# One GpSimd instruction for two states and two chunks in a selective-scan block

## The chip, the cores and the metric

The kernel runs on one core of one Trainium2 chip. The metric is the device time of one execution in microseconds (us), lower is better. Before the change it is 4063.8 us, the median of 3 runs (4062.99 to 4069.68).

## What is computed

The reference is a stack of four layers over `x` of 4 x 512 x 256 numbers, all in fp32: a cross-attention block, a transformer block with self- and cross-attention and a gated feed-forward part, a stack of four Mamba blocks over a 64-token prefix and the 512 tokens, and another transformer block. The change lies in the Mamba layer alone. Its core, cut down:

```python
def mamba_block(x, ip_w, cw, cb, xp_w, dtp_w, dtp_b, A_log, Dp, op_w):
    ...
    dt = jax.nn.softplus(jnp.einsum('bsr,er->bse', dt, dtp_w) + dtp_b)
    A = -jnp.exp(A_log)
    dA = jnp.exp(dt[..., None] * A)
    dBu = dt[..., None] * Bm[:, :, None, :] * xi[..., None]

    def step(h, t):
        da, dbu, c = t
        h = da * h + dbu
        return (h, jnp.einsum('bes,bs->be', h, c))
    ...
    y = ys.transpose(1, 0, 2) + xi * Dp
    y = y * jax.nn.silu(z)
    return jnp.einsum('bse,de->bsd', y, op_w)
```

`e` runs over 512 channels, `s` over 16 states, and there are four such blocks and four sequences.

## The kernel before

Layers 0 and 1 run first, with the 64 prefix tokens of the Mamba layer computed beside them; then comes the Mamba layer over the 512 tokens (`layer2`, called the scan block here), then layer 3. In the scan block the 512 channels are four chunks of 128 partitions, and time (512 steps) lies along the free dimension.

The work is cut into 16 units (4 blocks x 4 sequences). A unit has two pairs of chunks, a pair has 8 groups of two states, and a group has two chunks `k`. One pass `i` of the main loop, of 512, is one chunk of one group: `i = 32 n + 16 pair + 2 s2 + k`, and its group is `i // 2`. I call such a pass a slot. The order of all instructions is written out by hand (`tc.manual_schedule()`): each engine runs its own in program order, and waits only where data or a buffer demand it. A slot's steps:

- `maps`: SyncE loads the rows of B and C for two states, spread over 128 partitions (`bB`, 2 buffers, and `bC`, 4 buffers), 6 and 4 slots ahead.
- `decay` (L1706): ScalarE computes exp(dt A) of both states into PSUM (`ps_dA`, two buffers), one slot ahead.
- `product` (L1692): GpSimd multiplies dt x by B for one state and both chunks into `dBu` ([128, 2 states, 512, 2 chunks], chunks innermost, 3 buffers), three slots ahead. `begin` (L1711): ScalarE writes the first element of each state, from the state left by the prefix.
- `states` (L1718): VectorE scans both states of a chunk, reading `ps_dA` and, with a stride of two, `dBu`. The result goes back into `ps_dA`, or into an SBUF tile `hP` where GpSimd makes the output product.
- output products with C: `outputs_here` (L1723) on VectorE into `hC`, in the same slot, or `outputs` (L1727) on GpSimd in place in `hP`, one slot later. `on_gpsimd(i)` picks 13 slots in 32: the even ones without 10, 20 and 30. `hC` and `hP` share 6 buffers.
- `add_up` (L1749): TensorE transposes the products of a chunk by 8 matmuls with the identity, and thereby adds them up over the states in PSUM (`ps_y`), two slots later for VectorE's and three for GpSimd's. For a pair's first chunk 16 matmuls come before them (L1738, `dD` times `xi`, the term with D), which start the sums. `close_pair` (L1765) multiplies the sums by the gate on VectorE two slots after a pair's last chunk, into `g`.

Everything else of the layer is taken along by generators that `advance()` moves on twice a slot: `front` (norm, input projection `ps_in`, convolution `ps_cv`, `ps_x`, two units ahead), `step` (dt by `ps_dt`, softplus, `dtx`), `gate` (`ps_z`, into `zs`), `gated` (transposes of `g`, output projection `ps_out`, and the addition to `hT_res` on VectorE at L1633), and, in the last block, `tokens` (the final norm; L1667 on VectorE scales 256 columns with two operands in SBUF). They share two PSUM banks. `flush_silu` runs a silu on ScalarE, with its table loads, in slots 10 and 14 of a unit. The first part of the main loop's order:

```python
                    if main and i + 3 < NU * US:
                        product(i + 3)
                    if 0 <= i - 1 < NU * US:
                        outputs(i - 1)
                    ...
                    if main:
                        states(i)
                    ...
                    for j in (i - 3, i - 2):
                        if 0 <= j < NU * US and on_gpsimd(j) == (j == i - 3):
                            add_up(j)
```

Of the kernel before, what the change touches and what calls it, by code (L numbers as in the profile page):

```python
# [8 lines left out]
F32 = mybir.dt.float32  # L9
AF = mybir.ActivationFunctionType  # L10
ALU = mybir.AluOpType
# [4 lines left out]
P = 128  # L16
B = 4
T = 512
# [97 lines left out]
        return not (any(self.queues) or self.norms or self.pend or self.aside)  # L116


def on_gpsimd(i):

    return i % 2 == 0 and i % 32 not in (10, 20, 30)


@with_exitstack
def kernel(ctx: ExitStack, tc: tile.TileContext, t: dict, out: bass.AP):
    nc = tc.nc
# [1242 lines left out]
    def layer2(hT, A, far, h63, tail, X, fw, wl, late):  # L1369
# [5 lines left out]
        with ExitStack() as st:  # L1375
            pool = st.enter_context(tc.tile_pool(name="a2", bufs=1))
# [3 lines left out]
            NU = L * B  # L1380
            PS = 2 * (NS // 2)
            US = 2 * PS
# [40 lines left out]
            units = [{} for _ in range(NU)]  # L1423
# [248 lines left out]
            bmap, dBus, dAs, hCs, ysum = {}, {}, {}, {}, {}  # L1672

            def where(i):
                n, r = divmod(i, US)
                pair, r = divmod(r, PS)
                s2, k = divmod(r, 2)
                return n, pair, s2, k
# [5 lines left out]
                nc.sync.dma_start(out=tl, in_=units[n]["scr"][k, 2 * s2 : 2 * s2 + 2].partition_broadcast(P))  # L1684
                bmap[i // 2, k] = tl

            def product(i):
                n, pair, s2, j = where(i)
                dtx = units[n]["got", pair][1]
                if j == 0:  # L1690
                    dBus[i // 2] = pool.tile([P, 2, T, 2], F32, name="dBu", tag="dBu", bufs=3)
                nc.gpsimd.tensor_mul(  # L1692
                    dBus[i // 2][:, j, 1:, :],
                    dtx[:, 1:, :],
                    bmap[i // 2, 0][:, j, 1:].unsqueeze(2).broadcast_to([P, T - 1, 2]),
                )

            def decay(i, j):
# [6 lines left out]
                dt = units[n]["got", pair][0][:, k, :]  # L1705
                nc.scalar.activation(dA, dt, AF.Exp, scale=A[:, l, m, s : s + 1])  # L1706

            def begin(i):
                n, pair, s2, k = where(i)
                h0 = units[n]["got", pair][2]  # L1710
                nc.scalar.copy(dBus[i // 2][:, :, 0, :], h0[:, :, 2 * s2 : 2 * s2 + 2].rearrange("p k s -> p s k"))  # L1711

            def states(i):
                hCs[i] = hC = pool.tile([P, 2, T], F32, name="hP" if on_gpsimd(i) else "hC", tag="hC", bufs=6)
                dA = dAs[i].rearrange("p s t -> p (s t)")
                to = hC.rearrange("p s t -> p (s t)") if on_gpsimd(i) else dA
                dBu = dBus[i // 2].rearrange("p s t k -> p (s t) k")[:, :, i % 2]
                nc.vector.tensor_tensor_scan(to, dA, dBu, 0.0, ALU.mult, ALU.add)  # L1718

            def outputs_here(i):  # L1720
                dA = dAs.pop(i)
                if not on_gpsimd(i):
                    nc.vector.tensor_mul(hCs[i], dA, bmap[i // 2, 1])  # L1723

            def outputs(i):
                if on_gpsimd(i):
                    nc.gpsimd.tensor_mul(hCs[i], hCs[i], bmap[i // 2, 1])  # L1727

            def add_up(i):
                n, pair, s2, k = where(i)  # L1730
# [36 lines left out]
            def advance():  # L1767
                for gen in list(active):
                    try:
                        next(gen)  # L1770
                    except StopIteration:
                        active.remove(gen)
# [13 lines left out]
            with tc.manual_schedule():  # L1786
                for i in range(first, last):
                    n, r = divmod(i, US)
# [16 lines left out]
                    main = 0 <= i < NU * US  # L1805
# [3 lines left out]
                    for k, ahead in ((0, 6), (1, 4)):  # L1809
                        j = i + ahead  # L1810
# [8 lines left out]
                    if i == -1:  # L1819
                        product(0)  # L1820
                        product(1)
                        product(2)
                        begin(0)
                    if main and i + 3 < NU * US:
                        product(i + 3)
                    if 0 <= i - 1 < NU * US:
                        outputs(i - 1)

                    e = i - LAG
                    closing = 0 < e <= NU * US and e % PS == 0  # L1830
# [4 lines left out]
                    if main:  # L1835
                        states(i)
                    if closing:

                        advance()
                        advance()  # L1840
                    for j in (i - 3, i - 2):
                        if 0 <= j < NU * US and on_gpsimd(j) == (j == i - 3):
                            add_up(j)
                    if not closing:
                        advance()
                    if main:
                        outputs_here(i)
                    if main and i % 2 == 0 and i + 2 < NU * US:
                        begin(i + 2)
                    if not closing:  # L1850
                        advance()
                assert not active and len(banks) == 2
# [137 lines left out]
    with ExitStack() as st:  # L1990
        xp = st.enter_context(tc.tile_pool(name="X3", bufs=1))
        X = xp.tile([P, NT, D], F32, name="X")
        fw = row(xp, "l2_fw")
        wl = st.enter_context(tc.tile_pool(name="w2", bufs=1))
        wa = {}

        def late():

            wa["q"] = load_w(wl, "L3_q", [P, DC, 512], tag="inx")
            ko = wl.tile([P, 2, 1024], F32, name="w_ko", tag="dg")  # L2000
            wa["v"] = load_w(wl, "L3_v", [P, DC, D], tag="dD", bufs=2)
            for k, n in enumerate("ko"):
                wa[n] = ko[:, k, :].rearrange("p (c n) -> p c n", c=(DC, 4)[k])
                nc.sync.dma_start(out=wa[n], in_=t[f"L3_{n}"].rearrange("(c p) n -> p c n", p=P))

        layer2(hT, A, far[:, 0:2], h63, tail, X, fw, wl, late)
        layer3(X, wa, wl)
# [70 lines left out]
```

## Time and profile before

| | |
|---|---|
| median of 3 runs | 4063.8 us (4062.99 to 4069.68) |
| the profiled execution's own time | 4068.3 us |
| its span in the profile | 4066.5 us |
| granted TensorE clock | 0.914 |
| busy share of the span: PE, DVE, ACT, POOL | 86%, 72%, 53%, 60% |
| scan block | 1598 us to 3354 us after the start |
| input products on GpSimd (L1692) | 512 of 2136 ns |
| output products on GpSimd (L1727) | 208 of 2365 ns |
| scans on VectorE (L1718) | 304 of 2283 ns and 208 of 2279 ns |
| output products on VectorE (L1723) | 304 of 1223 ns |

The profile is of one execution. PE is TensorE's matmuls, PEld its weight loads, DVE VectorE, ACT ScalarE, POOL GpSimd, SP SyncE. A group of instructions has its line, engine and operation, what it writes and reads, shapes and count; after the bar stand its busy time, the mean ns of one, the idle time of the engine just before, and what ended that. A row of the waits has who waited, for whom, and the total, the times and the longest in us. A row of the timeline has start, length, engine, line, and the idle time before it in brackets. A line can be a helper's: TensorE's L190 and L183 are `matmul_k` and its version in halves.

### The profile page before, as it was taken

The page shows a single profiled execution, that of the slowest core. Times are in us where ns is not written, and L with a number is a line of the kernel's source. Part 1 is how long each engine was busy: PE and PEld are TensorE (multiplying, and loading weights), DVE is VectorE, ACT ScalarE, POOL GpSimd, SP SyncE. Part 2 cuts the span into 40 slices and gives each one's busy share as a digit, 9 for nine tenths or more (in the row PEclk, how much of TensorE's full clock was granted, in tenths as well). Part 3 has the DMA queues.
Part 4 walks back from the last instruction along what each step waited for, and adds up shares of the span by engine and source line. Part 5 has one row for each costly group of instructions (what it writes and reads, how often), then busy time and mean ns, then how long its engine had stood idle before and what let it go on. Part 6 is the DMA issues. An engine that isn't in the chain of part 4 may idle for free. (4 is left out here: it accounts for less than half of the span.)

```text
span 4066.5 us, 48201 instructions
## 1 busy us (share of the span) xinstructions
PE 3492.8 (86%) x17616; PEld 2200.1 (54%) x17616; DVE 2942.0 (72%) x2821; ACT 2156.9 (53%) x4106; POOL 2440.9 (60%) x1585
## 2 busy tenths in 40 slices
PE   7989998998888897888888888888888568999889
PEld 4654554544565554555555555555555444555446
DVE  5547567566565642889999989999999995676653
ACT  2345455454322433666767767666676643566422
POOL 3349269077100424899999999999999981000131
PEclk8999999999988998988988898889988778999999
DMA  2023022023100112444544545454444441000000
GB/s 77 12 87 104 25 81 96 18 90 104 45 1 0 54 31 70 151 157 154 164 166 156 162 157 176 156 163 156 164 158 146 152 142 41 1 1 1 1 6 16
DMA packets 140492, 370.30 MB, mean 91 GB/s; under 512 B 20640, under 2 KB 38240, under 8 KB 140256
## 3 DMA queue, kind: packets, MB, share of 16 engines
q1 hardware_dynamic: 136896, 363.98, 27.4%
q10 hardware_dynamic: 3360, 3.25, 0.3%
q8 instruction: 139, 2.28, 0.2%
q14 instruction: 97, 0.79, 0.1%
HBM read 363.89 MB, written 3.28 MB: 90 GB/s over the span
## 5 line engine op out<-in xcount | busy, mean ns | idle before, releaser
L1692 POOL TENSOR_TENSOR dBu<-dtx,bB 128x1022 f32<-128x1022 f32 x512 | 1084.7, 2136 | 13.0 <-DVE ps_dA L1718 5.9
L1706 ACT ACTIVATE ps_dA<-dt,A 128x512 f32<-128x512 f32 x1024 | 710.7, 694 | 358.1 <-DVE hC L1723 306.9
L1718 DVE TENSOR_TENSOR_SCAN ps_dA<-ps_dA,dBu 128x1024 f32<-128x1024 f32 x304 | 693.9, 2283 | 72.3 <-ACT ps_dA L1706 69.4
L1718 DVE TENSOR_TENSOR_SCAN hP<-ps_dA,dBu 128x1024 f32<-128x1024 f32 x208 | 474.1, 2279 | 58.9 <-POOL dBu L1692 49.8
L1727 POOL TENSOR_TENSOR hP<-hP,bC 128x1024 f32<-128x1024 f32 x208 | 491.9, 2365 | 26.9 <-DVE hP L1718 26.8
L1024 ACT ACTIVATE pr<-ps_s,nm 128x512 f32<-128x512 f32 x512 | 346.0, 688 | 259.8 <-DVE nm L1020 259.7
L1020 DVE TENSOR_REDUCE nm<-ps_s 128x2 f32<-128x1024 f32 x256 | 301.3, 1218 | 158.9 <-PE ps_s L1009 144.8
L1723 DVE TENSOR_TENSOR hC<-ps_dA,bC 128x1024 f32<-128x1024 f32 x304 | 371.7, 1223 | 17.9 <-PE ps_in L190 0.4
L1749 PE MATMUL ps_y<-ident,hC 128*128 128x128 f32 x2432 | 354.4, 296 | 27.3 <-DVE hC L1723 27.1
L1749 PE MATMUL ps_y<-ident,hP 128*128 128x128 f32 x1664 | 263.2, 311 | 110.7 <-POOL hP L1727 110.5
L1749 PEld LDWEIGHTS ps_y<-ident,hC 128*128 128x128 f32 x2432 | 309.9, 154 | 66.9 <-DVE hC L1723 41.8
L1038 PE MATMUL ps_pt<-ident,pr 128*128 128x128 f32 x2048 | 284.5, 279 | 66.8 <-DVE pT L1043 34.0
L1749 PEld LDWEIGHTS ps_y<-ident,hP 128*128 128x128 f32 x1664 | 227.5, 162 | 198.2 <-POOL hP L1727 140.7
L1038 PEld LDWEIGHTS ps_pt<-ident,pr 128*128 128x128 f32 x2048 | 231.9, 142 | 164.6 <-issue 60.6
L668 POOL TENSOR_TENSOR ln_rstd<-ln_rstd,const 128x4 f32<-128x4 f32 x24 | 24.4, 1017 | 446.3 <-DVE ln_rstd L667 444.8
L587 DVE TENSOR_TENSOR_SCAN phb<-pdA,phb 128x512 f32<-128x512 f32 x128 | 225.7, 1778 | 59.0 <-POOL phb L577 42.8
L183 PE MATMUL ps_cv<-xp,w_dg 128*128 128x512 f32 x512 | 239.2, 603 | 26.0 <-ACT xp L1501 19.6
L1041 ACT COPY pT<-ps_pt 128x512 f32<-128x512 f32 x256 | 140.7, 593 | 171.5 <-PE ps_pt L1038 171.1
L1057 PE MATMUL ps_o<-pT,V 128*64 128x256 f32 (+1 forms) x2048 | 221.8, 393 | 1.8 <-ACT AT L1075 1.8
L1009 PE MATMUL ps_s<-kT,qT 64*128 64x512 f32 (+1 forms) x1024 | 209.6, 647 | 2.2 <-DVE kT L1230 1.4
L577 POOL TENSOR_TENSOR phb<-hT_res,pm 128x512 f32<-128x512 f32 x128 | 187.8, 1471 | 34.2 <-DMA pm<-scrp 21.3
L840 POOL TENSOR_TENSOR pr<-pr,rs 128x512 f32<-128x512 f32 x64 | 65.4, 1042 | 218.2 <-DVE rs L838 212.3
(275 smaller groups left out, 6345.8 us busy)
## 6 DMA issues: line engine op xcount, KB each, us to landing
bB<-scr SPq DMA_DIRECT2D x256, 512.0 KB, 3.9
bC<-scr SPq DMA_DIRECT2D x256, 512.0 KB, 4.8
pm<-scrp SPq DMA_DIRECT2D x224, 256.0 KB, 3.1
w_pw_in<-in_L_in SPq DMA_DIRECT2D x7, 512.0 KB, 4.6
X<-in_x SPq DMA_DIRECT2D x4, 512.0 KB, 7.7
w_L_W<-in_L_W SPq DMA_DIRECT2D x2, 1024.0 KB, 10.0
w_L_Wq<-in_L_Wq SPq DMA_DIRECT2D x2, 1024.0 KB, 6.4
w_L_Wo<-in_L_Wo SPq DMA_DIRECT2D x2, 1024.0 KB, 8.9
```

The costliest lines, as they stand in the source:

```text
L183: nc.tensor.matmul(dst, l, r, start=(i == 0), stop=(i == len(pairs) - 1))
L587: nc.vector.tensor_tensor_scan(hb, dA, hb, 0.0, ALU.mult, ALU.add)
L1020: nc.vector.tensor_reduce(nm, ps, AX.X, ALU.max, negate=True)
L1024: nc.scalar.activation(pr, ps[:, x, :], AF.Exp, bias=nm[:, x : x + 1], accum_out=rs[:, y : y + 1])
L1038: nc.tensor.transpose(pp[:, t4, :], pr[:, t4 * P : (t4 + 1) * P], ident)
L1057: nc.tensor.matmul(ps_o[0][j * stride : (j + 1) * stride, half * W2 : (half + 1) * W2], Vs[n][0][:, t4, h * stride : (h + 1) * stride], pT ...
L1692: nc.gpsimd.tensor_mul(dBus[i // 2][:, j, 1:, :], dtx[:, 1:, :], bmap[i // 2, 0][:, j, 1:].unsqueeze(2).broadcast_to([P, T - 1, 2]),)
L1706: nc.scalar.activation(dA, dt, AF.Exp, scale=A[:, l, m, s : s + 1])
L1718: nc.vector.tensor_tensor_scan(to, dA, dBu, 0.0, ALU.mult, ALU.add)
L1723: nc.vector.tensor_mul(hCs[i], dA, bmap[i // 2, 1])
L1727: nc.gpsimd.tensor_mul(hCs[i], hCs[i], bmap[i // 2, 1])
L1749: nc.tensor.matmul(y[:, j, k * P : (k + 1) * P], hC[:, s, j * P : (j + 1) * P], ident, is_transpose=True, start=False, stop=(2 * s2 + s == ...
```

## The change

`product` and `outputs` now take a group `g` instead of a slot. One instruction makes both states and both chunks of an input product, with `dtx` repeated over the states and B over the chunks. Where a group is GpSimd's, the scans of both chunks write their states in place in `dBu`, and one instruction multiplies these by C, repeated over the chunks, also in place; TensorE's weight loads then read a chunk of `dBu` with a stride of two. `on_gpsimd` picks whole groups: 0, 2 and 4 of eight, and group 30 of 32, so 13 of 32. `dBu` has 4 buffers instead of 3, `hC` 4 instead of 6, and `hP` is gone. The input product of a group is issued in one slot, three before its first scan; the output product two slots after the group's first scan; GpSimd's chunks are added up four slots after their scan instead of three.

```diff
--- before.py
+++ after.py
@@ -116,9 +116,9 @@
         return not (any(self.queues) or self.norms or self.pend or self.aside)
 
 
-def on_gpsimd(i):
-
-    return i % 2 == 0 and i % 32 not in (10, 20, 30)
+def on_gpsimd(q):
+
+    return q % 8 in (0, 2, 4) or q % 32 == 30
 
 
 @with_exitstack
@@ -1684,15 +1684,13 @@
                 nc.sync.dma_start(out=tl, in_=units[n]["scr"][k, 2 * s2 : 2 * s2 + 2].partition_broadcast(P))
                 bmap[i // 2, k] = tl
 
-            def product(i):
-                n, pair, s2, j = where(i)
-                dtx = units[n]["got", pair][1]
-                if j == 0:
-                    dBus[i // 2] = pool.tile([P, 2, T, 2], F32, name="dBu", tag="dBu", bufs=3)
+            def product(g):
+                n, pair, s2, _ = where(2 * g)
+                dBus[g] = pool.tile([P, 2, T, 2], F32, name="dBu", tag="dBu", bufs=4)
                 nc.gpsimd.tensor_mul(
-                    dBus[i // 2][:, j, 1:, :],
-                    dtx[:, 1:, :],
-                    bmap[i // 2, 0][:, j, 1:].unsqueeze(2).broadcast_to([P, T - 1, 2]),
+                    dBus[g][:, :, 1:, :],
+                    units[n]["got", pair][1][:, 1:, :].unsqueeze(1).broadcast_to([P, 2, T - 1, 2]),
+                    bmap[g, 0][:, :, 1:].unsqueeze(3).broadcast_to([P, 2, T - 1, 2]),
                 )
 
             def decay(i, j):
@@ -1705,26 +1703,28 @@
                 dt = units[n]["got", pair][0][:, k, :]
                 nc.scalar.activation(dA, dt, AF.Exp, scale=A[:, l, m, s : s + 1])
 
-            def begin(i):
-                n, pair, s2, k = where(i)
+            def begin(g):
+                n, pair, s2, _ = where(2 * g)
                 h0 = units[n]["got", pair][2]
-                nc.scalar.copy(dBus[i // 2][:, :, 0, :], h0[:, :, 2 * s2 : 2 * s2 + 2].rearrange("p k s -> p s k"))
+                nc.scalar.copy(dBus[g][:, :, 0, :], h0[:, :, 2 * s2 : 2 * s2 + 2].rearrange("p k s -> p s k"))
 
             def states(i):
-                hCs[i] = hC = pool.tile([P, 2, T], F32, name="hP" if on_gpsimd(i) else "hC", tag="hC", bufs=6)
                 dA = dAs[i].rearrange("p s t -> p (s t)")
-                to = hC.rearrange("p s t -> p (s t)") if on_gpsimd(i) else dA
                 dBu = dBus[i // 2].rearrange("p s t k -> p (s t) k")[:, :, i % 2]
-                nc.vector.tensor_tensor_scan(to, dA, dBu, 0.0, ALU.mult, ALU.add)
+                nc.vector.tensor_tensor_scan(dBu if on_gpsimd(i // 2) else dA, dA, dBu, 0.0, ALU.mult, ALU.add)
 
             def outputs_here(i):
                 dA = dAs.pop(i)
-                if not on_gpsimd(i):
-                    nc.vector.tensor_mul(hCs[i], dA, bmap[i // 2, 1])
-
-            def outputs(i):
-                if on_gpsimd(i):
-                    nc.gpsimd.tensor_mul(hCs[i], hCs[i], bmap[i // 2, 1])
+                if not on_gpsimd(i // 2):
+                    hCs[i] = hC = pool.tile([P, 2, T], F32, name="hC", tag="hC", bufs=4)
+                    nc.vector.tensor_mul(hC, dA, bmap[i // 2, 1])
+
+            def outputs(g):
+                if on_gpsimd(g):
+                    h = dBus[g]
+                    nc.gpsimd.tensor_mul(h, h, bmap[g, 1].unsqueeze(3).broadcast_to([P, 2, T, 2]))
+                    for k in range(2):
+                        hCs[2 * g + k] = h[:, :, :, k]
 
             def add_up(i):
                 n, pair, s2, k = where(i)
@@ -1819,12 +1819,11 @@
                     if i == -1:
                         product(0)
                         product(1)
-                        product(2)
                         begin(0)
-                    if main and i + 3 < NU * US:
-                        product(i + 3)
-                    if 0 <= i - 1 < NU * US:
-                        outputs(i - 1)
+                    if main and i % 2 and i + 3 < NU * US:
+                        product((i + 3) // 2)
+                    if i % 2 == 0 and 0 <= i - 2 < NU * US:
+                        outputs((i - 2) // 2)
 
                     e = i - LAG
                     closing = 0 < e <= NU * US and e % PS == 0
@@ -1838,15 +1837,15 @@
 
                         advance()
                         advance()
-                    for j in (i - 3, i - 2):
-                        if 0 <= j < NU * US and on_gpsimd(j) == (j == i - 3):
+                    for j in (i - 4, i - 2):
+                        if 0 <= j < NU * US and on_gpsimd(j // 2) == (j == i - 4):
                             add_up(j)
                     if not closing:
                         advance()
                     if main:
                         outputs_here(i)
                     if main and i % 2 == 0 and i + 2 < NU * US:
-                        begin(i + 2)
+                        begin((i + 2) // 2)
                     if not closing:
                         advance()
                 assert not active and len(banks) == 2
```

## The prediction

> **What bounds the kernel now.** I read the slices first, then the windows, the groups of the scan block by shape, the waits of the same stretch, and last the timeline of a few slots. I call one pass `i` of the main loop a slot (512 of them) and 32 slots a unit.
>
> ```profile
> DVE  5547567566565642889999989999999995676653
> POOL 3349269077100424899999999999999981000131
> 1650.00:3100.00 1450.00, 1238.25 (x5703) 831.12 (x5704) 1328.13 (x783) 1011.66 (x1623) 1418.38 (x795) 0.87 0.49 159
> ```
>
> The slices place the scan block: first scan 1598 us, last 3354 us after the start. The window row gives, after its length, busy time of PE, PEld, DVE, ACT, POOL. Of 1450 us GpSimd works 1418 (97.8%), VectorE 1328 (91.6%), TensorE 1238 (85.4%). GpSimd looks like the bound.
>
> ```profile
> L1692 POOL TENSOR_TENSOR dBu<-dtx,bB 128x1022 f32<-128x1022 f32 x512 | 1084.7, 2136 | 13.0 <-DVE ps_dA L1718 5.9
> L1727 POOL TENSOR_TENSOR hP<-hP,bC 128x1024 f32<-128x1024 f32 x208 | 491.9, 2365 | 26.9 <-DVE hP L1718 26.8
> L577 POOL TENSOR_TENSOR phb<-hT_res,pm 128x512 f32<-128x512 f32 x128 | 187.8, 1471 | 34.2 <-DMA pm<-scrp 21.3
> ```
>
> ```profile
> DVE ps_dA L1718 <- ACT ps_dA L1706: 55.7, 55, 2.4
> DVE hT_res L1633 <- PE ps_out L183: 35.3, 26, 2.6
> DVE ps_dA L1718 <- POOL dBu L1692: 2.5, 3, 0.9
> PE ps_y L1749 <- POOL hP L1727: 64.9, 29, 3.9
> PE ps_y L1738 <- DVE g L1765: 41.5, 14, 4.1
> ```
>
> The waits (1650 to 3100 us; total, times, longest) say otherwise. VectorE waits 2.5 us for GpSimd's input products, but 55.7 for ScalarE's decays and 35.3 for TensorE. GpSimd's output products hold TensorE (64.9). So a faster GpSimd reaches the end only by way of TensorE. The timeline shows what TensorE does there:
>
> ```profile
> 2598.54 2.27 DVE L1718 TENSOR_TENSOR_SCAN ps_dA<-ps_dA,dBu 128x1024 f32<-128x1024 f32 x1
> ...
> 2601.41 1.04 PE L1749 MATMUL ps_y<-ident,hP 128*128 128x128 f32 x8
> ...
> 2602.28 1.04 PE L1749 MATMUL ps_y<-ident,hC 128*128 128x128 f32 x8
> 2603.16 1.88 PE L190 MATMUL ps_z<-w_inz,hn 128*128 128x512 f32 x4
> ...
> 2604.87 3.60 PE L183 MATMUL ps_out<-gT,w_out 128*128 128x512 f32 x8
> ...
> 2608.51 0.69 DVE L1633 TENSOR_TENSOR hT_res<-ps_out,hT_res 128x512 f32<-128x512 f32 x1 [2.05 <-PE ps_out L183]
> ```
>
> From slot 5 (scan at 2598.54) TensorE has no gap, is 2.9 us behind VectorE, and VectorE then waits 2.05 us for it. TensorE paces slots 3 to 9 of a unit and much of 17 to 31; VectorE and ScalarE pace 10 to 16.
>
> **The change, part by part.** The sum is made against the profiled execution: span 4066.5, its own time 4068.3, 4.5 us above the median of 4063.8. Units take 106.5 to 108.8 us (scan to scan, 32 apart), 115 in the two that hold the final norm. Some 15 units run steadily. A measurement of this kernel tells 0.2% (8 us) from no change.
>
> *GpSimd's instructions.* 512 input products become 256 of twice the size, 208 output products 104. Rows with two full operands give the fixed part: 251 ns at 32 elements (L1578) and 2365 at 1024, so 2.13 ns an element and 183 fixed. L1692, whose B is repeated over two chunks, leaves (2136-183)/1022 = 1.91 ns. The new input product is then 183+2044x1.91 = 4.09 us against 4.27, the new output product, with the same repeat, 4.10 against 4.73: 256x0.18+104x0.63 = 113 us less work. If nothing of the fixed part is saved it is 47. I take 113, as four row sizes lie on that line (L577's shortest, 1257 ns at 512, gives 1274). In the Trainium skill, GPSIMD Engine Reference, section 3.1, a two-input GpSimd operation of 2048 elements is listed at 4497 ns, with no gain for a repeated operand. By that page GpSimd would do about 35 us more instead of less (an estimate from the page), which speaks against the change; the 2136 ns of L1692 is already under half of the page's figure, so I follow the row. On the path I credit the 113 us with nothing: VectorE waited 2.5 us. What is late next is TensorE.
>
> *The buffer of a group on GpSimd.* The states stay in `dBu`, so it comes free after TensorE has added up the second chunk, not after VectorE's second scan. Input product g+4 takes the buffer of g: it is issued in slot 2g+5, and the add it needs opens slot 2g+5 on TensorE. This new wait of GpSimd on TensorE has the output product of g+2 and input product g+5 queued behind it, and for these TensorE, then VectorE (slot 2g+10), wait. In the timeline above the add that would free it ends at 2602.45, 3.9 us after slot 5 began. Then 4.09+4.10+4.09 and about 0.2 of handing over: input product 5 is there 16.4 us after slot 5. VectorE reached slot 10 at 2617.15, 18.6 us after; alone it would need 13.9 (three scans of 2.28, then two chunks at 3.5, in the new order). So in the first half of a unit TensorE's own pace covers the wait; where the cover is gone it costs up to 2.5 us. In slots 25 to 29, where TensorE starts 3.6 to 4.0 late, I count 0.5 us a unit: +8. Bounds 0 and +46 (3 us a unit).
>
> *Which groups go to GpSimd.* Before, even slots but 10, 20 and 30; after, both chunks of groups 0, 2, 4 of eight and one more in 32: 208 products either way. But slots 10 to 15 now all belong to VectorE, which had given away 12 and 14: two products of 1.22 us, +2.44 a unit, +37 over 15 units. Those that leave slots 5 and 9 lie where VectorE waits for TensorE, and bring nothing. Bounds 0 (later slots give it back) and +37; nearest is the stretch itself, which VectorE paces, so +37.
>
> *ScalarE.* At slot 14 a silu and two table loads delay the decay of slot 15; in every unit I looked at the scan there waits 1.75 us. Slot 14 becomes 1.22 longer, so this cover grows: -1.22x15 = -18. The softplus at slot 19 (1.08 us) keeps its distance, since slots 16 to 19 together are as long as before. Bounds 0 and -26.
>
> *The adds one slot later.* TensorE's first adds of a pair, with 16 matmuls before them that wait for `g` (41.5 us, 14 times), move from slot 3 to 4. Four `ps_z` matmuls (1.88 us) of slot 3 now fill that idle time, and the stretch behind it has no gap: -1.88x15 = -28. Bounds -45 (all idle time) and 0.
>
> *The final norm.* L1667 reads two SBUF operands and each of its instructions in the scan block ends with a GpSimd instruction: 9.37 us for four at 3211.93, 0.48 each once GpSimd is quiet. With GpSimd instructions of 4.1 us, four may take up to 16.4, +7 in each of three batches; VectorE's stop also stops GpSimd, so I take +5, +15. Bounds 0 and +21.
>
> *Costs I set at nothing.* The scans write with a stride of two: `hP` 2279 and `ps_dA` 2286 ns already differ only by 7, reads of `dBu` have this stride now, and L587 scans in place over its second input (1191 ns at 512 elements when alone). `hC` falls from 6 to 4 buffers: the fourth chunk back is added up two slots before, and TensorE is at most 6.2 us late. SP's loads are the same 512; the buffer of `bB` is free 4.1 us before its next use where two input products follow each other, landing takes 3.9, so at most some 0.5 us where GpSimd has time. ScalarE's `begin` waits for the same add as the input product, a slot later. TensorE's weight loads of GpSimd's 208 chunks are strided; no row has such a load. Bounded by none and by twice the present 8x0.13 us of a group: 0 to +216 of TensorE's time, half of it hidden at most. I take 0: VectorE and GpSimd rows show no price for this stride. In the Trainium skill, SBUF — State Buffer, under Door 1: The DMA port swizzle, fp32 may be strided within a 16-byte line without loss. No run here shows it for weight loads.
>
> Sum: 0+8+37-18-28+15 = +14 us, so 4082 for the profiled execution and 4063.8+14 = 4078 for the median.
>
> **The rivals.** *GpSimd's relief reaches the end* (faster). For it: 97.8% busy, and TensorE's 64.9 us of waits for output products in 1450. Over 15 units that is some 72 us; with the final norm's +15 it is -57, less what the burst costs: about -45, 4019. Against it: VectorE's own work and its table loads stay. It decides if TensorE's waits for GpSimd were what made it late in slots 17 to 31.
>
> *The new wait of GpSimd for TensorE sets the pace* (slower still). Price 3 us a unit, +46 on top of the +14: 4124. It decides when VectorE would cover slots 5 to 10 in under 16.4 us; 18.6 was measured, and every gain elsewhere brings it closer. Strided weight loads at a price add to the same queue.
>
> *The merged instruction saves nothing* (GpSimd's row stays proportional): GpSimd does 47 us less rather than 113; with credit zero the time stays near the forecast, 4080.
>
> **How the numbers follow.** Forecast with its bounds, the third rival in it, 0.45; relief reaches the end 0.28; the new wait decides 0.27. The forecast's own range is 4050 to 4110, of which I give 0.05 to faster by over 0.2%, 0.15 to within it, 0.25 to slower. Faster 0.28+0.05 = 0.33, same 0.15, slower 0.27+0.25 = 0.52. The range reaches from 4018 (relief) to 4135 (new wait and something of the strided loads); about 0.08 is left out below, 0.1 above.
>
> **What would show it.** L1692's successor at 4.09 us x256 and the output product at 4.10 x104 show the first step; 4.27 or 4.5 shows it wrong. POOL waiting for `PE ps_y` is the new buffer wait; tens of us on VectorE for `dBu` mean that it sets the pace. VectorE's wait at slot 15 should fall to 0.5 us, TensorE's wait for `g` by half, L1667 rise to some 3.5 us. Weight loads of `dBu` above 0.16 us would show a price of the stride. The forecast is wrong if units fall under 106 us or rise over 110.

## The result, and the profile after

| | before | after |
|---|---|---|
| median, same chip | 4063.39 us (4 runs, 4062.29 to 4069.68) | 4119.64 us (4 runs, 4118.49 to 4122.01) |
| ratio, 95% interval | | 1.0136 [1.0118, 1.0153] |
| the profiled execution's own time, span | 4068.3, 4066.5 us | 4122.0, 4120.0 us |
| granted TensorE clock | 0.914 | 0.908 |

The kernel became slower by 56 us. The page of the changed kernel, the slices of VectorE and GpSimd first, then groups of the scan block (busy time, mean ns of one, idle time before and what ended it):

```profile
DVE  5548577576555633898989888988898996766653
POOL 3349168076100425898888988898988881000131
...
L1690 POOL TENSOR_TENSOR dBu<-dtx,bB 128x2044 f32<-128x2044 f32 x256 | 1042.7, 4086 | 46.8 <-DMA bB<-scr 31.2
...
L1725 POOL TENSOR_TENSOR dBu<-dBu,bC 128x2048 f32<-128x2048 f32 x104 | 425.3, 4089 | 162.3 <-issue 120.6
L1714 DVE TENSOR_TENSOR_SCAN dBu<-ps_dA,dBu 128x1024 f32<-128x1024 f32 x208 | 465.1, 2273 | 56.9 <-POOL dBu L1690 49.0
...
L1749 PEld LDWEIGHTS ps_y<-ident,hC 128*128 128x128 f32 x2432 | 311.6, 156 | 145.9 <-DVE hC L1720 130.1
...
L1749 PEld LDWEIGHTS ps_y<-ident,dBu 128*128 128x128 f32 x1664 | 233.7, 209 | 106.5 <-issue 56.8
```

In the scan block the rows of nines of VectorE and of GpSimd are now eights and nines. The two GpSimd instructions last what the sum gave them. GpSimd has less to do (2343.7 us against 2440.9 in the whole span) and now stands idle longer before them: 46.8 and 162.3 us, against 13.0 and 26.9 in the prediction's lines. The window of 1650 to 3100 us shows the same (length, then busy time of PE, PEld, DVE, ACT, POOL, then the granted clock):

```profile
1650.00:3100.00 1450.00, 1215.12 (x5506) 803.57 (x5505) 1286.61 (x754) 972.63 (x1563) 1288.66 (x476) 0.86 0.47 155
```

GpSimd fell from 1418 to 1289 us, but VectorE fell too, from 1328 to 1287, and its work per unit has not shrunk. So VectorE stands longer. The waits of that stretch say for whom (total, times, longest):

```profile
DVE ps_dA L1714 <- ACT ps_dA L1704: 65.9, 76, 4.4
...
PE ps_rb L1472 <- POOL rstd L1465: 54.4, 12, 9.4
...
PE ps_z L190 <- ACT zs L1600: 41.3, 10, 4.8
...
DVE hT_res L1633 <- PE ps_out L183: 39.6, 13, 3.5
...
POOL dBu L1690 <- DMA bB<-scr: 26.4, 13, 2.6
...
DVE g L1765 <- PE ps_y L1749: 22.3, 9, 5.6
...
DVE hn L1479 <- PE ps_rb L1472: 11.5, 4, 2.9
...
PE ps_y L1749 <- POOL dBu L1725: 6.5, 7, 1.5
```

TensorE's wait for GpSimd's output products is nearly gone (64.9 to 6.5), and its wait for `g` (41.5) is not in the list any more. In their place stand a wait for ScalarE's `zs` and one for GpSimd's `rstd`, the small root of the norm. The view of before has for these:

```profile
PE ps_rb L1472 <- POOL rstd L1465: 18.1, 3, 6.0
...
PE ps_z L190 <- ACT zs L1600: 10.9, 13, 2.9
```

The largest new wait of TensorE, 66.2 us for VectorE's `hC` (9.7 before), is not what slows the kernel: in the faster version with earlier adds, below, it is 79.0. VectorE waits longer for three results of TensorE: for `hT_res` 39.6 us against 35.3, for `g` 22.3 against 9.3, for `hn` 11.5 where there was none.

Two tables worked out from the traces, means of eight steady units (slots 96 to 352), in us, with the scan block as a whole in the last column of the first; the experiments are explained below:

| kernel | unit | VectorE busy | GpSimd busy | scan block |
|---|---|---|---|---|
| before | 107.5 | 98.8 | 105.9 | 1755.9 |
| after | 111.7 | 99.1 | 99.8 | 1806.1 |
| groups only | 111.9 | 99.1 | 106.1 | 1801.0 |
| inputs only | 107.3 | 98.8 | 103.5 | 1750.4 |
| after, adds earlier | 108.4 | 99.0 | 99.7 | 1760.8 |
| the same, 14 of 32 | 106.3 | 97.5 | 101.8 | 1734.3 |
| before, 14 of 32 | 110.0 | 97.7 | 108.2 | 1778.7 |

VectorE's idle time is a unit less its busy time: 8.7 us before, 12.6 after. That difference is the slowdown (3.9 us of the 4.2 a unit).

The second table shows where in a unit the time lies: how long VectorE takes from one scan to a later one. The first row has the lengths before, the others how much longer or shorter each stretch is.

| kernel | slots 0-5 | 6-7 | 8-9 | 10-15 | 16-27 | 28-29 | 30-31 | unit |
|---|---|---|---|---|---|---|---|---|
| before | 19.4 | 8.2 | 6.9 | 20.2 | 39.3 | 6.5 | 7.1 | 107.5 |
| after | 0.0 | +3.4 | -1.9 | +2.6 | +0.1 | 0.0 | 0.0 | +4.2 |
| groups only | +1.1 | +0.5 | -1.8 | +2.6 | -0.3 | +2.3 | +0.1 | +4.4 |
| groups only, 12 of 32 | +0.4 | +0.8 | -1.9 | +2.8 | -0.3 | +2.5 | 0.0 | +4.3 |
| after, root left out | +0.3 | +3.0 | -1.9 | +2.7 | -0.8 | -0.5 | 0.0 | +2.7 |
| after, opening matmuls earlier | +0.3 | +1.6 | -1.9 | +2.6 | -0.3 | -0.3 | 0.0 | +2.0 |
| after, adds earlier | -0.1 | +0.2 | -1.9 | +2.6 | -0.1 | +0.1 | 0.0 | +0.9 |
| the same, groups spread | 0.0 | +0.2 | +0.5 | +0.2 | -0.3 | +0.1 | 0.0 | +0.8 |
| adds earlier, 14 of 32 | -1.0 | 0.0 | -1.9 | +1.3 | -0.1 | +0.5 | 0.0 | -1.2 |

The change lengthens two stretches. Slots 6 and 7 hold VectorE's longest wait for TensorE's `ps_out`; in slots 10 to 15 VectorE now makes all the products, and slots 8 and 9 give most of that back.

### The profile page after: what moved, and what is told of

Its sections match the earlier page's. It is cut to its first block, busy times and chain, and to the rows that moved or that the text cites. A ratio compares the mean times of both kernels' runs of the same rounds, so it can differ in the third digit from the quotient of the medians.

```text
span 4120.0 us, 47410 instructions
## 1 busy us (share of the span) xinstructions
PE 3508.2 (85%) x17616; PEld 2197.0 (53%) x17616; DVE 2940.4 (71%) x2821; ACT 2151.2 (52%) x4106; POOL 2343.7 (57%) x1225
## 5 line engine op out<-in xcount | busy, mean ns | idle before, releaser
L1690 POOL TENSOR_TENSOR dBu<-dtx,bB 128x2044 f32<-128x2044 f32 x256 | 1042.7, 4086 | 46.8 <-DMA bB<-scr 31.2
L1714 DVE TENSOR_TENSOR_SCAN ps_dA<-ps_dA,dBu 128x1024 f32<-128x1024 f32 x304 | 696.1, 2290 | 88.3 <-ACT ps_dA L1704 88.2
L1725 POOL TENSOR_TENSOR dBu<-dBu,bC 128x2048 f32<-128x2048 f32 x104 | 425.3, 4089 | 162.3 <-issue 120.6
L1714 DVE TENSOR_TENSOR_SCAN dBu<-ps_dA,dBu 128x1024 f32<-128x1024 f32 x208 | 465.1, 2273 | 56.9 <-POOL dBu L1690 49.0
L1749 PE MATMUL ps_y<-ident,hC 128*128 128x128 f32 x2432 | 363.4, 299 | 92.8 <-DVE hC L1720 92.2
L1749 PEld LDWEIGHTS ps_y<-ident,dBu 128*128 128x128 f32 x1664 | 233.7, 209 | 106.5 <-issue 56.8
L1749 PE MATMUL ps_y<-ident,dBu 128*128 128x128 f32 x1664 | 247.5, 294 | 45.6 <-POOL dBu L1725 45.6
L190 PE MATMUL ps_z<-w_inz,hn 128*128 128x512 f32 x256 | 150.0, 717 | 77.9 <-ACT zs L1600 49.1
```

Of the source, the lines that this page charges most:

```text
L190: nc.tensor.matmul(dst, a, b, start=(i == 0), stop=(i == n - 1))
L1690: nc.gpsimd.tensor_mul(dBus[g][:, :, 1:, :], units[n]["got", pair][1][:, 1:, :].unsqueeze(1).broadcast_to([P, 2, T - 1, 2]), bmap[g, 0][:, ...
L1714: nc.vector.tensor_tensor_scan(dBu if on_gpsimd(i // 2) else dA, dA, dBu, 0.0, ALU.mult, ALU.add)
L1725: nc.gpsimd.tensor_mul(h, h, bmap[g, 1].unsqueeze(3).broadcast_to([P, 2, T, 2]))
L1749: nc.tensor.matmul(y[:, j, k * P : (k + 1) * P], hC[:, s, j * P : (j + 1) * P], ident, is_transpose=True, start=False, stop=(2 * s2 + s == ...
```

## The experiments

Ratios are against the kernel before on the same chip, with 95% intervals. The whole change is +56 us by the medians; 0.001 is 4.07 us.

**Only the distribution.** The kernel before with one line changed: GpSimd takes whole groups; all instructions, slots and buffers stay.

```diff
 def on_gpsimd(i):
-    return i % 2 == 0 and i % 32 not in (10, 20, 30)
+    q = i // 2
+    return q % 8 in (0, 2, 4) or q % 32 == 30
```

> The kernel before with one line changed: whole groups (0, 2, 4 of eight and 30 of 32) give their output products to GpSimd, instead of every second slot. All instructions keep their old size. Theory A (the new distribution over the slots is what costs: VectorE's run of slots 10 to 15, two short slots in a row elsewhere): most of the +56 us appears, 4095 to 4120. Theory B (the doubled GpSimd instructions cost, by what is queued behind them): within 10 us of before, 4055 to 4075.

Measured: 4116.07 us, 1.0115 [1.0098, 1.0132], +47. The waits of this run:

```profile
DVE ps_dA L1719 <- ACT ps_dA L1707: 85.9, 63, 4.9
...
PE ps_cv L184 <- POOL xp L1497: 43.4, 22, 3.4
```

The second line stands at 1.8 us before, and in the waits of after TensorE's matmuls have no such entry. The timeline from slot 27 to slot 30 of a unit shows it (start, length, engine, line, idle time before in brackets; L1693 is the input product, L1728 the output product):

```profile
2473.24 2.13 POOL L1693 TENSOR_TENSOR dBu<-dtx,bB 128x1022 f32<-128x1022 f32 x1
...
2475.32 2.36 POOL L1728 TENSOR_TENSOR hP<-hP,bC 128x1024 f32<-128x1024 f32 x1
...
2477.62 0.20 POOL L1497 COPY xp<-tail 128x3 f32<-128x3 f32 x1
...
2477.87 5.37 PE L184 MATMUL ps_cv<-xp,w_dg 128*128 128x512 f32 x8 [2.73 <-POOL xp L1497]
...
2483.28 0.69 ACT L1489 ACTIVATE xi<-ps_cv,cols 128x512 f32<-128x512 f32 x1 [5.60 <-PE ps_cv L184]
2483.86 1.41 ACT L1707 ACTIVATE ps_dA<-dt,A 128x512 f32<-128x512 f32 x2
...
2485.36 2.30 DVE L1719 TENSOR_TENSOR_SCAN ps_dA<-ps_dA,dBu 128x1024 f32<-128x1024 f32 x1 [4.87 <-ACT ps_dA L1707]
```

Input and output products follow each other on GpSimd without a gap (two are shown), and a copy of three elements, 0.20 us long, has to wait in order behind them. TensorE's convolution waits 2.73 us for the copy, ScalarE's `xi` 5.60 for the convolution, and the next decay, in order behind `xi`, is late: VectorE's scan in slot 30 waits 4.87 us for it. Over the eight units this wait is 3.06 us a unit, against 0.76 before; it is 4.8 to 4.9 in the four units where slots 28 and 29 are GpSimd's, so that VectorE comes early, and 0.5 to 2.0 in the others. By the second table slots 28 and 29 take 2.3 us longer, about half of this run's +4.4 a unit. That the copy is the cause is read from the chain; no run moves the copy alone. Slots 0 to 7 add 1.6 us and slots 10 to 15 2.6, and slots 8 and 9 give 1.8 back.

**One group fewer on GpSimd, the same order.** In the kernel of the first experiment, 12 groups of 32 instead of 13.

```diff
-    q = i // 2
-    return q % 8 in (0, 2, 4) or q % 32 == 30
+    return i // 2 % 8 in (0, 2, 4)
```

> As e1 (old instructions, whole groups), with 12 groups in 32 instead of 13: GpSimd has 2.4 us a unit less, VectorE 1.2 more. If e1 is slow because GpSimd, in its runs, cannot keep up and idles between them, 10 to 35 us under e1: 1.003 to 1.009 of before. If e1 is slow because of VectorE's run of slots 10 to 15, slower than e1: 1.013 to 1.018.

Measured: 4117.74 us, 1.0118 [1.0096, 1.0141], no different from 13. GpSimd's work fell by 2.4 us a unit and VectorE's rose by 1.2, and neither moved the end. TensorE's wait for the copy stayed at 42.5 us. In the four units that had group 30 on GpSimd, slots 28 and 29 take 9.2 to 9.4 us in both runs, though VectorE makes two products more there, 2.4 us, in the second. So what is lost in these slots is set neither by GpSimd's load nor by VectorE's, which leaves the order of the queues. Of slots 10 to 15 this run says nothing: VectorE's products there are the same in both. The step is one group in two units, it relieves one engine and loads the other, and an effect of less than some 8 us would lie within the intervals.

**Only the merged input product.** The kernel before with `product` of the change, three buffers, and the outputs, the slots and the adds as they were.

```diff
-            def product(i):
-                n, pair, s2, j = where(i)
+            def product(g):
+                n, pair, s2, _ = where(2 * g)
...
-                    if main and i + 3 < NU * US:
-                        product(i + 3)
+                    if main and i % 2 and i + 3 < NU * US:
+                        product((i + 3) // 2)
```

> The kernel before with the input product of a group as one instruction; output products, their slots, buffers and adds as before. Theory A: GpSimd does 47 us less and nothing is moved, so 4045 to 4065. Theory B: GpSimd's small steps (the norm's root, the tails) now wait behind 4.1 us instructions, and the time rises, 4075 to 4110.

Measured: 4062.27 us, 0.9984 [0.9975, 0.9993], -7. GpSimd does 2.4 us less a unit, and the unit is 0.2 shorter.

**The adds a slot earlier.** The changed kernel with GpSimd's chunks added up three slots after their scan, as before the change.

```diff
-                    for j in (i - 4, i - 2):
-                        if 0 <= j < NU * US and on_gpsimd(j // 2) == (j == i - 4):
+                    for j in (i - 3, i - 2):
+                        if 0 <= j < NU * US and on_gpsimd(j // 2) == (j == i - 3):
```

> The changed kernel with GpSimd's chunks added up three slots after their scan, as before the change, instead of four. If the later adds (and the 16 matmuls before them) make TensorE late for g and for the output projection, 10 to 25 us come back, 4095 to 4110. If TensorE then waits for the doubled output product instead, it is slower, 4125 to 4150. Theory A expects little, 4110 to 4130.

Measured: 4071.74 us, 1.0006 [0.9997, 1.0015]. One slot of delay in the adds is worth 53 us (1.0136 less 1.0006), nearly all of the slowdown. It lies in one place: of the 3.3 us a unit between the two versions 3.2 are in slots 6 and 7. Its waits, to be set beside those of after:

```profile
PE ps_rb L1472 <- POOL rstd L1465: 26.2, 3, 9.0
...
PE ps_y L1738 <- DVE g L1765: 19.5, 13, 2.1
...
DVE hT_res L1633 <- PE ps_out L183: 12.9, 13, 2.1
DVE g L1765 <- PE ps_y L1749: 12.5, 3, 4.3
...
PE ps_z L190 <- ACT zs L1600: 7.6, 8, 1.9
```

TensorE waits for `g` again, 19.5 us; VectorE's wait for `hT_res` is a third of 39.6. How a longer wait at one place can be the better one is seen in the first slots of one unit. The changed kernel, whose unit begins with the scan at 2726.31:

```profile
2726.31 4.46 DVE L1714 TENSOR_TENSOR_SCAN dBu<-ps_dA,dBu 128x1024 f32<-128x1024 f32 x2
...
2731.53 1.88 PE L190 MATMUL ps_z<-w_inz,hn 128*128 128x512 f32 x4
...
2733.68 1.95 PE L1738 MATMUL ps_y<-w_dD,xi 128*128 128x128 f32 x16
...
2740.17 1.42 ACT L1704 ACTIVATE ps_dA<-dt,A 128x512 f32<-128x512 f32 x2 [1.80 <-DVE hC L1720]
...
2741.52 0.58 ACT L1600 COPY zs<-ps_z 128x512 f32<-128x512 f32 x1
...
2742.15 3.78 PE L190 MATMUL ps_z<-w_inz,hn 128*128 128x512 f32 x4 [3.08 <-ACT zs L1600]
...
2743.96 4.07 POOL L1690 TENSOR_TENSOR dBu<-dtx,bB 128x2044 f32<-128x2044 f32 x1
...
2746.57 1.91 PE L1749 MATMUL ps_y<-ident,dBu 128*128 128x128 f32 x8
...
2754.56 0.69 DVE L1633 TENSOR_TENSOR hT_res<-ps_out,hT_res 128x512 f32<-128x512 f32 x1 [3.50 <-PE ps_out L183]
```

And the same unit with the adds a slot earlier, from its scan at 2699.94:

```profile
2699.94 4.46 DVE L1714 TENSOR_TENSOR_SCAN dBu<-ps_dA,dBu 128x1024 f32<-128x1024 f32 x2
...
2705.83 3.48 PE L1738 MATMUL ps_y<-w_dD,xi 128*128 128x128 f32 x16 [1.32 <-DVE g L1765]
...
2713.82 1.13 PE L1749 MATMUL ps_y<-ident,dBu 128*128 128x128 f32 x8
...
2715.35 0.58 ACT L1600 COPY zs<-ps_z 128x512 f32<-128x512 f32 x1
...
2715.98 1.98 PE L190 MATMUL ps_z<-w_inz,hn 128*128 128x512 f32 x4 [0.16 <-ACT zs L1600]
...
2724.46 0.69 DVE L1633 TENSOR_TENSOR hT_res<-ps_out,hT_res 128x512 f32<-128x512 f32 x1 [0.48 <-PE ps_out L183]
```

ScalarE copies `zs` 15.2 us after the unit's first scan in the one and 15.4 in the other. That time is given: the copy stands behind a decay that waits for VectorE (1.80 us in both). TensorE's second `ps_z` can't come before it, since a bank has to be free. With early adds TensorE does the opening matmuls, the first `ps_z` and the adds of both chunks of group 0 (the second at 2713.82) before that moment, and waits 0.16 us. With late adds the first `ps_z` has moved ahead of the opening matmuls, as I had predicted, but the adds of the second chunk now stand behind the second `ps_z`. TensorE waits 3.08 us with them in its queue, does them afterwards, and `ps_out` and the addition to `hT_res` come 28.3 us after the unit's first scan instead of 24.5 (over the eight units 29.2 against 26.0, and 25.8 in the kernel before). The changed line moved work from in front of a wait to behind it.

TensorE also runs slower behind that wait. The window rows of after and of the version with early adds (after the length the busy times, with counts in brackets, then the granted clock):

```profile
2742.00:2746.00 4.00, 3.85 (x6) 1.68 (x7) 4.00 (x3) 2.08 (x7) 3.92 (x5) 0.50 0.38 119
```

```profile
2714.00:2718.00 4.00, 3.84 (x22) 2.60 (x22) 4.00 (x2) 3.84 (x8) 3.92 (x5) 1.00 0.02 7
```

At a clock of 0.50, then 0.60 (2746 to 2749 us), the four `ps_z` matmuls take 3.78 us against 1.98, and the eight adds 1.91 against 1.13. So of the 3.7 us by which `hT_res` is later in this unit 2.6 are slower matmuls, and 1.1 the adds themselves. The version with early adds has its slow stretch too (the opening matmuls take 3.48 us after a wait of 1.32, against 1.95), but it lies before the copy of `zs`, where it costs nothing here. That the longer wait brings the lower clock was not tried by itself: after the same wait of 2.73 us the eight convolution matmuls of the first experiment took 5.37 us in the unit shown and 3.70 in the next.

**Only the 16 opening matmuls earlier.** The changed kernel, adds still four slots after the scan; only the matmuls that open a pair come a slot earlier.

```diff
-            def add_up(i):
+            def open_pair(i):
...
+                    if 0 <= i - 3 < NU * US:
+                        open_pair(i - 3)
                     for j in (i - 4, i - 2):
```

> The changed kernel, adds four slots after the scan, but the 16 matmuls that open a pair's sums three slots after its first scan, as before the change. If the later place of these 16 is what makes TensorE late for the output projection, most of the 53 us between the changed kernel and e4 come back: 4070 to 4090. If the adds themselves, each a slot later, are what costs, 4105 to 4120.

Measured: 4091.99 us, 1.0067 [1.0052, 1.0082]. Of the 53 us some 28 belong to these matmuls and some 25 to the adds themselves; by the scan blocks of the profiled executions (1760.8 with all early, 1777.9 here, 1806.1 after) it is 28 and 17. VectorE's waits here:

```profile
DVE hT_res L1633 <- PE ps_out L183: 26.6, 13, 3.0
...
DVE g L1769 <- PE ps_y L1753: 22.3, 9, 5.6
```

The wait for `hT_res` lies half way between 12.9 and 39.6, and slots 6 and 7 are 1.6 us longer than before, between 0.2 and 3.4: both parts of the delay reach VectorE there. That for `g` is the same as in after, so it comes with the late adds and not with the opening matmuls.

**The groups spread out, adds earlier.** Thirteen groups of 32, two or three apart, in the kernel with the early adds.

```diff
-    return q % 8 in (0, 2, 4) or q % 32 == 30
+    return q % 32 in (0, 2, 5, 8, 10, 13, 16, 18, 21, 24, 26, 28, 30)
```

> As e4 (adds three slots after the scan), 13 groups in 32 on GpSimd, but 0, 2, 5 of eight instead of 0, 2, 4 (with 28 and 30 at the end of 32): VectorE's run in slots 10 to 15 of the first half shrinks to 12 to 15. If that run is what the grouping costs (2.44 us a unit), 15 to 35 us under e4: ratio to before 0.992 to 0.997. If the cost lies in GpSimd's own bursts, about as e4, 0.998 to 1.004.

Measured: 4072.21 us, 1.0019 [1.001, 1.0028]. Nothing is gained by it: slots 10 to 15 take 2.4 us less than in the version with early adds, and slots 8 and 9 take 2.4 more.

**The root left out.** The changed kernel without GpSimd's step for the root of the scan block's norm.

```diff
-                nc.vector.tensor_scalar(rstd, ps[:, :TPB], EPS, None, ALU.add)
+                nc.vector.tensor_scalar(rstd, ps[:, :TPB], 0.0, 0.001, ALU.mult, ALU.add)
...
-                nc.gpsimd.tensor_tensor(rstd, rstd, mhalf, ALU.pow)
```

> The changed kernel without the inverse root of the scan block's norm: VectorE writes a constant in its place, GpSimd has no such step. TensorE waited 54.4 us for that step in the changed kernel between 1650 and 3100 us (18.1 before). Theory B: 30 to 50 us come back, 4070 to 4090. Theory A: that wait is mostly beside the path, at most 15 us, 4105 to 4120.

Measured: 4099.06 us, 1.0073 [1.0058, 1.0088]. This gives back 26 of the 56 us. It has not been tried in the kernel before, where TensorE waited 18.1 us for the root instead of 54.4. But TensorE needs the root around slots 19 and 23 of VectorE, and by the second table slots 16 to 31 are no longer after the change than before (+0.1); without the root they are 1.4 us a unit shorter. So little of the 26 us can be part of the change's net cost.

**A contiguous output product.** The kernel with the early adds, the output product written chunk by chunk into a tile of its own, so that the weight loads are not strided. That tile has one buffer and `dBu` three.

```diff
-                    h = dBus[g]
-                    nc.gpsimd.tensor_mul(h, h, bmap[g, 1].unsqueeze(3).broadcast_to([P, 2, T, 2]))
+                    h = pool.tile([P, 2, 2, T], F32, name="hP", tag="hP", bufs=1)
+                    nc.gpsimd.tensor_mul(
+                        h.rearrange("p k s t -> p s t k"), dBus[g], bmap[g, 1].unsqueeze(3).broadcast_to([P, 2, T, 2])
+                    )
```

> As e4, but GpSimd's output product writes a tile of its own with each chunk contiguous (one buffer; dBu with 3 buffers), so that TensorE's weight loads have no stride. These loads went from 162 to 209 ns and the 8 matmuls of a state pair from 1.04 to 1.12 us. If the stride costs the path something, 5 to 18 us under e4: 0.996 to 0.9995 of before. If not, 0.999 to 1.003.

Measured: 4069.84 us, 1.0011 [1.0001, 1.002], the same as 1.0006 within the intervals. A group of its page:

```profile
L1751 PEld LDWEIGHTS ps_y<-ident,hP 128*128 128x128 f32 x1664 | 213.0, 155 | 160.8 <-POOL hP L1725 119.3
```

The load is back at 155 ns from 209, and the end does not move. GpSimd waits more here before its input products, 74.5 us for VectorE's scans with three buffers of `dBu` (5.4 for the one buffer of `hP`), so a small gain could be hidden.

**A larger share for GpSimd.** Fourteen of 32 in the kernel with early adds, then fifteen, and for comparison fourteen in the kernel before and in the one with merged inputs only.

```diff
-    return q % 8 in (0, 2, 4) or q % 32 == 30
+    return q % 16 in (0, 2, 4, 6, 8, 10, 12)
```

> As e4, with group 6 of the first half of each unit on GpSimd as well (14 in 32): VectorE has 1.22 us less in slots 12 and 13, GpSimd 4.09 more in every second pair, 2 us a unit on average. If VectorE's run in slots 10 to 15 is on the path, 0.990 to 0.997 of before; if GpSimd is, 1.000 to 1.010.

```diff
-    return q % 16 in (0, 2, 4, 6, 8, 10, 12)
+    return q % 16 in (0, 2, 4, 6, 8, 10, 12) or q % 32 == 30
```

> As e7, with group 30 of 32 too: 15 groups in 32 on GpSimd, adds three slots after the scan. GpSimd was idle 4.7 us a unit in e7 and gets 2 us more, VectorE 1.2 us less. If VectorE is still on the path, 0.990 to 0.995 of before; if GpSimd's bursts or TensorE are, 0.996 to 1.003.

In the kernel before and in the one with merged inputs:

```diff
-    return i % 2 == 0 and i % 32 not in (10, 20, 30)
+    return i % 2 == 0 and i % 32 not in (10, 20)
```

> The kernel before with slot 30 of 32 on GpSimd too (14 in 32), all else as before. GpSimd was busy 98.5% of steady units and gets 2.37 us a unit more, VectorE 1.22 less. If GpSimd's load bounds the kernel before, slower: 1.003 to 1.010. If VectorE does, 0.993 to 0.999.

> As e2 (only the input products merged, 47 us less for GpSimd), and slot 30 of 32 on GpSimd too (14 in 32). If the relief of GpSimd is worth what is moved onto it, 0.990 to 0.997 of before; if the slots' own order and TensorE bound it by now, 0.997 to 1.003.

Measured: 4044.7 us, 0.9954 [0.9937, 0.997] for fourteen, some 19 us under the kernel before; 4052.93, 0.9959 [0.9944, 0.9974] for fifteen, no further gain; 4088.05, 1.0047 [1.003, 1.0063] for the kernel before with fourteen; 4076.16, 1.0017 [1.0004, 1.0029] with merged inputs. The fourteenth brings 21 us with both products merged, and costs 19 without. But it does not lie in the same place: the merged version gives group 6, slots 12 and 13 of every unit, to GpSimd and takes group 30 back, and slots 10 to 15 become 1.3 us a unit shorter; the other two versions give slot 30 to GpSimd. Where the step is slot 30 or group 30 in all, it costs 19 us with nothing merged, 13 with merged inputs (0.9984 to 1.0017), and 2, within the intervals, with both merged (fourteen to fifteen). So merging makes the step cheaper, and the gain of 21 us belongs to the place as well. The window and two waits of the merged fourteen:

```profile
1650.00:3100.00 1450.00, 1206.95 (x5733) 821.73 (x5732) 1329.24 (x778) 1018.03 (x1629) 1378.85 (x506) 0.90 0.49 162
```

```profile
PE ps_y L1749 <- POOL dBu L1725: 122.0, 33, 8.2
...
DVE hT_res L1633 <- PE ps_out L183: 9.5, 13, 2.2
```

GpSimd works 1379 us of 1450. In the kernel before with fourteen it works 1422, and VectorE has begun to wait for its input products, 15.0 us against 2.8 with thirteen:

```profile
DVE hP L1718 <- POOL dBu L1692: 15.0, 20, 1.9
```

In the faster version TensorE waits 122 us for output products, against 6.5 in after, and yet VectorE waits only 9.5 for `hT_res`. I read this as follows: a wait of TensorE costs where something that VectorE needs soon is queued behind it, and little elsewhere.

## Why the prediction was right or wrong

Slower was forecast and slower was measured, 42 us above the figure. But of the sum's larger terms only some held, and errors of both signs offset each other, so that the sign and the nearness of the figure are in part luck.

**The instructions: right.** 4.09 and 4.10 us predicted, 4086 and 4089 ns measured; GpSimd's busy time fell by 97 us in the page, and by 109 on its two lines (1576.6 to 1468.0), against 113. The Trainium skill's figure in GPSIMD Engine Reference, section 3.1 (4497 ns for 2048 elements with two inputs) does not hold for these operands, one of which is repeated: 4089 ns was measured, and the row of the profile before was the better guide.

**The adds one slot later: the step that failed, in sign.** I set -28 us, for four matmuls that would fill TensorE's wait for `g`, "and the stretch behind it has no gap". They filled it: the wait for `g` vanished. But the run with the early adds puts the step at +53. The stretch behind did have a wait to offer, the one for `zs`, which was small before (10.9 us in 1450), with enough work in front of it. The adds of the second chunk now stand behind that wait, and behind it TensorE runs at a lower clock, which the sum did not have either; in the unit shown these make 1.1 and 2.6 us. VectorE pays in slots 6 and 7, 3.2 us a unit. I counted the idle time that goes and did not ask which wait of the same queue comes next, and what then stands behind it.

**Which groups go to GpSimd: right at the place, near in size by luck.** I set +37, 2.44 us a unit, for two products in the slots 10 to 15 that VectorE paces, and this stretch became 2.6 us longer. But what leaves slots 5 and 9 was to bring nothing, and slots 8 and 9 give 1.8 us back (1.9 in after). The one-line experiment gives +47 all the same, because 2.3 us a unit come up in slots 28 and 29, which the sum does not name, at the end of a chain that begins with a three-element copy in GpSimd's in-order queue; the rest comes up in slots 0 to 7.

**GpSimd's relief, credited with nothing: wrong for this kernel.** In the old distribution the credit was near the truth: merged inputs alone bring 7 us. With whole groups the merged products bring 44 (1.0115 to 1.0006, the other differences being the place of the states, the slot of the output product and the numbers of buffers): TensorE's wait for the small copy, 43.4 us, is gone, and slots 28 and 29 are back at +0.1 from +2.3. The relief has a second use that the sum did not ask for: a further group on GpSimd, number 30, costs 2 us, within the intervals, instead of 19.

Taken in this order the steps are grouping +47, merging -44 and the later adds +53. They lead from the one kernel to the other and so must add up to the result; in another order the parts differ, as the 7 us of the merged inputs show. What does not depend on the order is the place: of after's +4.2 us a unit 3.4 lie in slots 6 and 7, and slots 8 to 15 have the other 0.7.

**The buffer wait of GpSimd on TensorE: did not happen.** I charged +8, and the second rival +46, for input product g+4 waiting for the adds of group g. In the timeline of after, the product at 2743.96 is that of group 4, and the second chunk of group 0 is added up at 2746.57: the product does not wait for it. Over the trace 96 of 102 such products start before those adds end, by 1.8 to 6.1 us (medians, by the place in eight). So the product cannot have that buffer; it must take one that is already free, such as that of one of VectorE's groups. The waits of 1650 to 3100 us hold no entry of GpSimd for `ps_y`. So the second rival's time, 4124, is close to the measured one, but its mechanism is not what happened; VectorE does wait longer for TensorE, but for another reason.

**ScalarE: right at the place, lost elsewhere.** The scan's wait in slot 15 fell from 1.75 to 0.38 us a unit (-1.37; -1.22 predicted). New waits of VectorE for ScalarE's decay appeared in slots 11 (1.21) and 7 (0.98), so that slots 10 to 15 became 2.6 us longer and not the 1.2 that the two terms make together.

**The final norm: sign wrong.** I expected L1667 at some 3.5 us each and +15.

```profile
L1667 DVE SCALAR_TENSOR_TENSOR X<-X,ss,row_l_fw x16: 452/474/4289, 3156.7 to 3427.3; 128x256 f32<-128x256 f32 x16
```

The longest are as long as I thought, 4289 ns, but the median is 474. In the three batches of the scan block the four instructions together last 9.5, 4.3 and 4.2 us; before, 6.9, 9.6 and 9.6. Before, 11 of these 12 ran beside an instruction of GpSimd and ended just after one; after, only 4 did, for 2.8 to 4.3 us, and the other eight took 452 to 472 ns. So the single wait is longer, as I thought, and there are fewer, which I had not thought of. The two units that hold the norm became 5.6 us longer together (121.2 and 114.2 after, 115.0 and 114.8 before), less than two ordinary ones did (8.4).

**What I set at nothing.** The scans: 2273 and 2290 ns, no price of the stride. The input product's wait for the load of `bB` was to be "at most some 0.5 us": it is 26.4 us in 13 times, 2.0 each; it lies where GpSimd has idle time, and whether it costs was not tried by itself. The weight loads of `dBu` took 209 ns against 156 for `hC` in the same profile, so the stride has a price there; in the contiguous version, where it is gone, the end did not move. The price for weight loads differs from the Trainium skill's SBUF — State Buffer, under Door 1: The DMA port swizzle, by which fp32 strided inside a 16-byte line costs nothing; here the measurement decides.

Still open: by which waits grouping alone lengthens slots 0 to 7, whether the copy alone makes slots 28 and 29 longer, and what brings the lower clock behind TensorE's waits.

## What to carry to other kernels

On an engine with a fixed order, moving a step later moves it past every wait that its queue holds, so before an idle gap is credited, ask which wait comes next and what will then stand behind it. An engine that is 98% busy may be worth little by its total and much by its order: about half of 47 us came up at the end of a chain that begins with a 0.2 us copy behind large instructions, where the relief alone brought 7. A relief that brings little by itself can make room for more work on the relieved engine (number 30 of 32 cost 19 us in the kernel before, and 2 with both products merged and the early adds), so try the share again after such a change, and the place of the share with it. To find where a change costs, compare the lengths of the same stretches of the loop; the table of slots said more here than the totals of the waits.

## What was not expected of the hardware

- TensorE's weight load from a chunk with a stride of two fp32 elements took 209 ns, contiguous 155 to 156; eight adds in the shown unit of the version with early adds took 1.13 us against 1.04 for contiguous ones. The run without the stride was no faster.
- VectorE's L1667, which reads two operands from SBUF, took 0.48 us where GpSimd was quiet and up to 4289 ns beside a 4.1 us instruction of GpSimd. That single instructions grew was expected, not that the three batches of the scan block together fell from 26.0 to 18.0 us.
- TensorE's granted clock was 0.50 for 4 us behind a wait of 3.08 us, and four matmuls took 3.78 us instead of 1.98.
